# Four-layer graph network on one core: graph 0's masks on VectorE, its attention rows made by TensorE, four output tiles beside the p's

## The chip, the cores and the metric

The kernel runs on one core of one Trainium2 chip. Times are device microseconds of that core. Five engines work side by side, each through its own instructions in their order: TensorE (PE, with its weight loads PEld), VectorE (DVE), ScalarE (ACT), GpSimd (POOL) and SyncE (SP, which here only issues DMAs). They wait for each other by semaphores.

## The reference

Sixteen graphs of N = 1024 nodes with D = 256 features go through four layers; `adj` is a symmetric 0/1 matrix with ones on the diagonal.

```python
    h = jnp.maximum(_layernorm(x, axis=-1), 0.0)
    x = x + _L0_gnn_ref(h, adj, L0_gnn_W, L0_gnn_a)     # and so on for layers 1 to 3

    def _L0_gnn_ref(input, adj, W, a):
        h = jnp.matmul(input, W)
        f1 = jnp.einsum('bnf,f->bn', h, a1)
        f2 = jnp.einsum('bnf,f->bn', h, a2)
        e = jax.nn.leaky_relu(f1[:, :, None] + f2[:, None, :], negative_slope=ALPHA)
        logits = jnp.where(adj > 0, e, NEG_BIG)
        attention = jax.nn.softmax(logits, axis=1)
        return jax.nn.elu(jnp.matmul(attention, h))
```

Layer 1 is the same with the softmax along the other axis. Layer 2 averages projected neighbours; layer 3 has four attention heads of 64 features and a normalization per head. The change touches what layers 0 and 1 do for the first graph.

## The kernel before

Two programs are in the kernel: a fast one, and a general one behind a flag that these inputs don't raise. Only the fast one runs. Each graph is a Python generator, `graph(b)`: it normalizes x (`Norm`), runs `layer0` to `layer3`, and hands its end to `tail`. The generators yield planned times. A queue at the end of the program always resumes the one whose planned time is least, with 120 us between graphs, and so sets the order in which the instructions are traced. From that order a planner with its own idea of durations makes each engine's order: it may put an instruction that it takes to be ready ahead of earlier ones. `later(...)` pins an instruction behind what was traced before it on its engine. All SP loads and rows are pinned.

Every layer treats nodes in NT = 8 tiles of 128.

- **Norm** (L599 to L681): statistics on VectorE (L631, or sums from `residual` and squares on ScalarE, L640), 1/std on POOL (L592, L593), the normalized and clipped rows hn on ScalarE (L667), transposes on TensorE (L680, called flips here), copied to ht (L681).
- **Mask** (L548): the transposed adjacency comes as int32 pieces `raw` of 128x512, 256 KB each, three buffers, sixteen pieces a graph, loaded by SP (L566). ScalarE squares each into bytes and sums it (L575).
- **layer0** (L742): eight projections of 258 columns (L686), copied to hs on ScalarE (L746). The last two columns are f1 and f2 of each node. The f1's, one per partition, must become a row that stands in all 128 partitions: `column` gathers them on VectorE (L717), `spread` transposes them on TensorE (L699), takes the exps (L703) and writes them to DRAM (L705), and `everywhere` reads them back with a broadcast (L711). Layer 0 needs two such rows (scales 1 and 0.2). Then come the eight p's: two VectorE operations over 128x1024 each (L769 and L771, the second with the mask), a reciprocal, and hs scaled by it on ScalarE (L773). Output tile i needs all eight p's: eight products (L759) into one PSUM bank. EARLY = 2 tiles are multiplied beside the p's, and up to p 6 their products are pinned; the other six tiles follow. For each tile ScalarE takes exp and a copy (L791, L793) and VectorE adds to x (L736, L737).
- **layer1** (L798) is alike, with one row, one VectorE operation per p (L822), products of 257 columns (L815), and e and v in L838 and L840.
- **layer2** and **layer3**: products L877, L883 and L942; p's L929.

PSUM has four pools of two banks: tr (transposes), mm (projections, weight preparation), at (output tiles of layers 0 and 1), hd (output tiles of layers 2 and 3). The SBUF tag `e` has two buffers.

The loads that graph 0 does not need at once wait behind its p's: `behind(t)` copies one element of the p that was traced last (`gates[-1]`, L484) into the tile to be loaded. `more()` traces them in three steps: the weights of layer 1 (`weights01`, with a small preparation on TensorE, L507, and copies L511), of layer 2 with the biases (L521 scales beta on VectorE), and of layer 3 (L534 to L536). The x of graphs 1 and 2 waits in the same way.

Of the kernel before, what the change touches and what calls it, by code (L numbers as in the profile page):

```python
# [8 lines left out]
F32 = mybir.dt.float32  # L9
U8 = mybir.dt.uint8  # L10
AF = mybir.ActivationFunctionType
OP = mybir.AluOpType
AX = mybir.AxisListType

P = 128
# [406 lines left out]
def tile_simple_stack(  # L422
# [11 lines left out]
    nc = tc.nc  # L434
    B, N, D = x.shape
# [4 lines left out]
    HALF = 512  # L440
    NHALF = N // HALF
    PER = NT // NHALF
    EIGHTH = 128
    NE = N // EIGHTH
    S, S3 = 0.2, 0.01
# [3 lines left out]
    EARLY = 2  # L449

    const = ctx.enter_context(tc.tile_pool(name="const", bufs=1))
# [9 lines left out]
    ident = const.tile([P, P], F32)  # L461
    make_identity(nc, ident)
    neg_half = const.tile([P, NT * H], F32)
    nc.vector.memset(neg_half, -0.5)
    unread = const.tile([P, D], U8)

    state = ctx.enter_context(tc.tile_pool(name="state", bufs=2))
    work = ctx.enter_context(tc.tile_pool(name="work", bufs=2))
# [24 lines left out]
    wx, rows = {}, {}  # L493
# [54 lines left out]
    class Mask:  # L548
# [4 lines left out]
        def __init__(self, b):  # L553
            self.b, self.next, self.raws = b, 0, []
            self.bytes = None
            for _ in range(self.AHEAD):
                self.load()
# [11 lines left out]
        def step(self, count=1):  # L569
            if self.bytes is None:  # L570
                self.bytes = state.tile([P, NT, N], U8, tag="mask", name="mask")
            for _ in range(count):
                s, n, g, raw = self.raws.pop(0)
                k = self.b * NT * NHALF + s
                nc.scalar.activation(  # L575
                    self.bytes[:, n, g * HALF : (g + 1) * HALF], raw, AF.Square, accum_out=squares[:, k : k + 1]
                )
                self.load()

    def load_adj(b, g):  # L580
# [108 lines left out]
    def new_hs(name="hs"):  # L689
        return state.tile([P, NT, W3], F32, tag="hs", name=name, bufs=3)  # L690

    def spread(col, n, scales, name):

        k = n * NT
        ps = tr_ps.tile([P, P], F32, tag="tr", name="ps_col")
        nc.tensor.transpose(ps[:k, :], col, ident)  # L699
        all_rows = []  # L700
        for scale in scales:
            e = small.tile([H * NT, P], F32, tag="e_row", name="e_row", bufs=2)
            nc.scalar.activation(e[:k, :], ps[:k, :], AF.Exp, scale=scale)  # L703
            d = dram.tile([n, N], F32, tag=f"row_{name}", name="d_row", bufs=4)
            later(nc.sync.dma_start(d.rearrange("r (t p) -> (r t) p", p=P), e[:k, :]))  # L705
            all_rows += [d[r] for r in range(n)]
        return all_rows

    def everywhere(d, tag):
        row = work.tile([P, N], F32, tag=tag, name="row", bufs=2)  # L710
        later(nc.sync.dma_start(row, d.partition_broadcast(P)))  # L711
        return row

    def column(src, n):

        col = small.tile([P, H, NT], F32, tag="col", name="col", bufs=2)
        nc.vector.tensor_copy(col[:, :n, :], src.rearrange("p t n -> p n t"))  # L717
        return col[:, :n, :].rearrange("p n t -> p (n t)")
# [22 lines left out]

    def layer0(b, xs, m, norm, after):  # L742
        hs = new_hs()
        for n in range(NT):
            ps = project(norm, wx[0], n, D + 2)
            nc.scalar.activation(hs[:, n, : D + 2], ps[:, : D + 2], AF.Copy, scale=norm.rs[n])  # L746
            m.step()
            yield 0.98
        mask = m.bytes
        row_a, row_b = [everywhere(d, "row") for d in spread(column(hs[:, :, D : D + 1], 1), 1, (1.0, S), "l0")]  # L750
        q = small.tile([P, NT], F32, tag="q", name="q")
        nc.scalar.activation(q, hs[:, :, D + 1], AF.Exp, scale=1.0 - S)
        watch(b, 0, hs[:, :, D : D + 2])
        yield 5.42
        ps_ = []
        early = [at_ps.tile([P, HALF], F32, tag="at", name="ps_o0") for _ in range(EARLY)]

        def product(ps, i, j):
            m = nc.tensor.matmul(  # L759
                ps[:, :D], ps_[j][:, i * P : (i + 1) * P], hs[:, j, :D], start=(j == 0), stop=(j == NT - 1)  # L760
            )
            if i < EARLY and j < 7:
                later(m)

        for j in range(NT):
            if m.raws:
                m.step(2)
            p = weights("p0")
            nc.vector.scalar_tensor_tensor(p, row_a, q[:, j : j + 1], row_b, op0=OP.mult, op1=OP.max)  # L769
            z = small.tile([P, 2], F32, tag="z", name="z", bufs=8)  # L770
            nc.vector.scalar_tensor_tensor(p, p, 1.0, mask[:, j, :], op0=OP.mult, op1=OP.mult, accum_out=z[:, 0:1])  # L771
            nc.vector.reciprocal(z[:, 1:2], z[:, 0:1])
            nc.scalar.activation(hs[:, j, :D], hs[:, j, :D], AF.Copy, scale=z[:, 1:2])  # L773
            ps_.append(p)
            if b == 0:
                gates.append(p)
            for i, ps in enumerate(early):
                if j:
                    product(ps, i, j - 1)
            yield 2.7  # L780
        for i, ps in enumerate(early):
            product(ps, i, NT - 1)
        for i in range(NT):
            if i < EARLY:
                ps = early[i]
            else:
                ps = at_ps.tile([P, HALF], F32, tag="at", name="ps_o0")
                for j in range(NT):
                    product(ps, i, j)
            e = work.tile([P, D], F32, tag="e", name="e")  # L790
            nc.scalar.activation(e, ps[:, :D], AF.Exp)  # L791
            v = work.tile([P, D], F32, tag="v", name="v")
            nc.scalar.copy(v, ps[:, :D])  # L793
            residual(xs, i, v, after, e)
            yield 3.74


    def layer1(b, xs, mask, norm, after):  # L798
        hs = new_hs()
        for n in range(NT):  # L800
            ps = project(norm, wx[1], n, D + 2)
            nc.scalar.activation(hs[:, n, : D + 2], ps[:, : D + 2], AF.Copy, scale=norm.rs[n])
            yield 1.05
        (d_row,) = spread(column(hs[:, :, D + 1 : D + 2], 1), 1, (S - 1.0,), "l1")
        row = everywhere(d_row, "row")
        watch(b, 1, hs[:, :, D : D + 2])
        q = small.tile([P, NT], F32, tag="q", name="q")
        nc.scalar.activation(q, hs[:, :, D], AF.Exp, scale=1.0 - S)
        nc.scalar.activation(hs[:, :, D], hs[:, :, D], AF.Exp, scale=S)
        yield 8.0  # L810
        ps_ = []
        early = [at_ps.tile([P, HALF], F32, tag="at", name="ps_o1") for _ in range(EARLY)]

        def product(ps, i, j):
            nc.tensor.matmul(  # L815
                ps[:, : D + 1], ps_[j][:, i * P : (i + 1) * P], hs[:, j, : D + 1], start=(j == 0), stop=(j == NT - 1)
            )

        for j in range(NT):
            nc.scalar.activation(hs[:, j, :D], hs[:, j, :D], AF.Copy, scale=hs[:, j, D : D + 1])  # L820
            p = weights("p1")
            nc.vector.scalar_tensor_tensor(p, row, q[:, j : j + 1], mask[:, j, :], op0=OP.max, op1=OP.mult)  # L822
            ps_.append(p)
            for i, ps in enumerate(early):
                product(ps, i, j)
            yield 1.35
        for i in range(NT):
            if i < EARLY:
                ps = early[i]
            else:  # L830
                ps = at_ps.tile([P, HALF], F32, tag="at", name="ps_o1")
                for j in range(NT):
                    product(ps, i, j)
            k = b * NT + i
            z = shares[:, k : k + 1]
            nc.vector.reciprocal(z, ps[:, D : D + 1])
            e = work.tile([P, D], F32, tag="e", name="e")
            nc.scalar.activation(e, ps[:, :D], AF.Exp, scale=z)  # L838
            v = work.tile([P, D], F32, tag="v", name="v")
            nc.scalar.activation(v, ps[:, :D], AF.Copy, scale=z)  # L840
            residual(xs, i, v, after, e)
            yield 3.74
# [186 lines left out]
    def loads(b):  # L1029
        loaded[b] = load_x(b)  # L1030
        yield 30.0
        masks[b] = Mask(b)
        yield 0
# [3 lines left out]
    def more():  # L1037

        weights01(1, w1, w1_t, a1, (1, 0))
        yield 21.6  # L1040
        weights2()
        yield 9.2
        weights3()
        yield 0
# [2 lines left out]
    next(loads_0)  # L1047
    weights01(0, w0, w0_t, a0, (0, 1), wait=False)
    next(loads_0)
    queue = [(36, 0, more())] + [(b * APART, b, graph(b)) for b in range(B)] + [(b * APART - 60, b, loads(b)) for b in range(1, B)]  # L1050
    while queue:
        queue.sort(key=lambda g: g[:2])
        at, b, g = queue.pop(0)
# [86 lines left out]
```

## Time and profile before

| | |
|---|---|
| median of 3 runs | 2623.5 us (2618.03 to 2626.04) |
| span of the profiled execution | 2619.6 us |
| TensorE busy | 2456.4 us, 94% |
| VectorE, ScalarE busy | 1965.3 us (75%), 1439.9 us (55%) |
| TensorE busy in the first 156 us | 109.9 us |
| TensorE busy in 313 to 470 us | 152.8 us of 157 |
| mean granted TensorE clock | 0.986 |

The span runs from the first to the last instruction of one execution taken by the profiler; the page gives no other time of that execution, and its span lies inside the runs' own spread. A line of the timeline gives the start, how long the instructions took, engine, line and operation, what is written and read, and how often; in brackets the engine's idle time before it and what ended that. A busy TensorE means that instructions are in it, not that it is at its best: their ends are modelled.

### The profile page before, as it was taken

Reading aid. Unit: us, or ns where it says so; the run is one execution under the profiler, and the core shown is the slowest. Engines: PE = TensorE matmul, PEld = TensorE weight load, DVE = VectorE, ACT = ScalarE, POOL = GpSimd, SP = SyncE. Lnnn points to the kernel's source line nnn. Section 1 sums busy time; section 2 is a strip of 40 time slices with the busy share of each in tenths; the row PEclk is TensorE's granted clock in tenths of the full one; section 3 lists DMA queues with packets and bytes.
Section 4 is the critical chain, followed back from the end, with each engine's and each line's share of the span. In section 5 each row is a group of like instructions: output and inputs, shape, how many; then the busy total and the mean of one; then the engine's idle time right before and its main releaser. Section 6 shows DMA issues by size and latency. Waiting matters only on the chain.

```text
span 2619.6 us, 63024 instructions
## 1 busy us (share of the span) xinstructions
PE 2456.4 (94%) x26194; PEld 2094.9 (80%) x26194; DVE 1965.3 (75%) x3815; ACT 1439.9 (55%) x4065; POOL 449.5 (17%) x454
## 2 busy tenths in 40 slices
PE   5799999999999999999999999999999999999975
PEld 4688888888878888787888878888888888878864
DVE  4457778687687977778687787877778687787858
ACT  4564755637565473755637565473755637565350
POOL 1010211203112030211203112030211203011021
PEclk8899999999999999999999999999999999999997
DMA  4541442616225251331615225251432615224021
GB/s 144 126 85 54 107 85 62 133 59 144 53 76 126 70 133 55 108 83 62 134 58 144 57 76 122 70 133 54 124 67 64 137 59 140 66 71 101 26 65 36
DMA packets 212632, 233.76 MB, mean 89 GB/s; under 512 B 10416, under 2 KB 161072, under 8 KB 212336
## 3 DMA queue, kind: packets, MB, share of 16 engines
q1 hardware_dynamic: 74608, 145.73, 17.5%
q0 software_dynamic: 137728, 83.90, 17.5%
q8 instruction: 208, 3.41, 0.5%
q14 instruction: 88, 0.72, 0.1%
HBM read 212.35 MB, written 17.24 MB: 88 GB/s over the span
## 4 chain that ended last, share of the span: by engine, by line
PE 56%; DVE 16%; DMA 12%; ACT 11%; issue 3%; POOL 2%; SPq 0%; DVEq 0%; POOLq 0%; ACTq 0%
PE ps_o L759 15%; PE ps_proj L686 12%; PE ps_o L942 9%; DVE p L929 6%; PE ps_o L883 6%; PE ps_o L815 6%; DMA row<-d_row 5%; PE pt_h L680 5%; DMA raw<-in_adj_t 4%; DVE p L822 4%; ACT mask L575 3%; PE ps_o L877 3%; ACT hn L667 2%; DMA d_row<-e_row 2%; ACT unread L640 2%
## 5 line engine op out<-in xcount | busy, mean ns | idle before, releaser
L929 DVE SCALAR_TENSOR_TENSOR p<-row,q,mask 128x1024 f32<-128x1024 f32 x512 | 631.9, 1278 | 65.4 <-PE ps_o L942 55.7
L942 PEld LDWEIGHTS ps_o<-hb,p 128*64 128x64 f32 x16384 | 505.5, 138 | 102.0 <-DVE p L929 41.2
L942 PE MATMUL ps_o<-hb,p 128*64 128x65 f32 x16384 | 541.6, 224 | 28.9 <-DVE p L929 20.8
L759 PE MATMUL ps_o<-hs,p 128*128 128x256 f32 x2048 | 494.0, 386 | 26.4 <-ACT hs L773 26.0
L686 PE MATMUL ps_proj<-wx,ht 128*128 128x258 f32 (+2 forms) x2048 | 507.8, 388 | 4.0 <-ACT hs L746 2.3
L815 PE MATMUL ps_o<-hs,p 128*128 128x257 f32 x2048 | 494.3, 388 | 14.5 <-ACT mask L575 7.7
L759 PEld LDWEIGHTS ps_o<-hs,p 128*128 128x128 f32 x2048 | 379.7, 191 | 82.8 <-ACT hs L773 30.3
L815 PEld LDWEIGHTS ps_o<-hs,p 128*128 128x128 f32 x2048 | 373.9, 190 | 69.9 <-ACT mask L575 8.3
L686 PEld LDWEIGHTS ps_proj<-wx,ht 128*128 128x128 f32 x2048 | 365.8, 190 | 79.6 <-ACT hs L746 10.4
L592 POOL TENSOR_SCALAR rs<-mv 128x4 f32<-128x4 f32 (+1 forms) x112 | 40.6, 362 | 1555.3 <-ACT unread L640 1542.1
L593 POOL TENSOR_TENSOR rs<-rs,neg_half 128x4 f32<-128x4 f32 (+2 forms) x144 | 261.6, 1818 | 11.7
L736 DVE SCALAR_TENSOR_TENSOR xs<-e,xs 128x256 f32<-128x256 f32 x256 | 108.0, 422 | 182.2 <-ACT e L791 134.1
L667 ACT ACTIVATE hn<-xs,shift 128x256 f32<-128x256 f32 x384 | 175.3, 502 | 123.6 <-DVE shift L635 123.6
L680 PE MATMUL pt_h<-ident,hn 128*128 128x128 f32 x1024 | 180.9, 287 | 43.4 <-ACT hn L667 42.4
L575 ACT ACTIVATE mask<-raw 128x512 uint8<-128x512 int32 x256 | 160.1, 627 | 86.7 <-DMA raw<-in_adj_t 59.5
L883 PE MATMUL ps_o<-hi,adj 128*128 128x258 f32 x1024 | 202.9, 321 | 1.6
L680 PEld LDWEIGHTS pt_h<-ident,hn 128*128 128x128 f32 x1024 | 115.1, 142 | 111.1 <-ACT hn L667 95.0
L585 POOL DMA_DIRECT2D adj<-in_adj x128 | 114.6, 896 | 480.3 <-PE ps_o L883 478.6
L737 DVE SCALAR_TENSOR_TENSOR xs<-v,xs 128x256 f32<-128x256 f32 x384 | 161.0, 422 | 29.5 <-ACT v L793 16.2
L769 DVE SCALAR_TENSOR_TENSOR p<-row,q 128x1024 f32<-128x1024 f32 x128 | 161.4, 1270 | 25.1 <-DMA row<-d_row 25.1
L950 ACT ACTIVATE res<-ps_o 128x260 f32<-128x260 f32 x128 | 46.5, 375 | 228.0 <-PE ps_o L942 227.7
L822 DVE SCALAR_TENSOR_TENSOR p<-row,q,mask 128x1024 f32<-128x1024 f32 x128 | 156.9, 1279 | 10.3 <-DMA row<-d_row 10.1
(108 smaller groups left out, 3000.1 us busy)
## 6 DMA issues: line engine op xcount, KB each, us to landing
raw<-in_adj_t SPq DMA_DIRECT2D x256, 256.0 KB
adj<-in_adj POOLq DMA_DIRECT2D x128, 512.0 KB, 4.9
row<-d_row SPq DMA_DIRECT2D x112, 512.0 KB
xs<-in_x POOLq DMA_DIRECT2D x32, 512.0 KB, 7.1
out<-xs SPq DMA_DIRECT2D x32, 512.0 KB
wx<-in_w SPq DMA_DIRECT2D x3, 256.0 KB
d_row<-e_row SPq DMA_DIRECT2D x48, 4.0 KB
wts<-in_w_t SPq DMA_DIRECT2D x2, 256.0 KB
```

What stands on the lines that cost most here:

```text
L575: nc.scalar.activation(self.bytes[:, n, g * HALF : (g + 1) * HALF], raw, AF.Square, accum_out=squares[:, k : k + 1])
L593: nc.gpsimd.tensor_tensor(rs[:, :n], rs[:, :n], neg_half[:, :n], op=OP.pow)
L667: nc.scalar.activation(hn, xs[:, 2 * g + k, :], AF.Relu, scale=scale, bias=bias)
L680: nc.tensor.transpose(pt[:, c, k * P : (k + 1) * P], hn[:, c * P : (c + 1) * P], ident)
L686: nc.tensor.matmul(ps[:, :width], norm.ht[:, c, n * P : (n + 1) * P], w[:, c, :width], start=(c == 0), stop=(c == DC - 1))
L759: m = nc.tensor.matmul(ps[:, :D], ps_[j][:, i * P : (i + 1) * P], hs[:, j, :D], start=(j == 0), stop=(j == NT - 1))
L769: nc.vector.scalar_tensor_tensor(p, row_a, q[:, j : j + 1], row_b, op0=OP.mult, op1=OP.max)
L815: nc.tensor.matmul(ps[:, : D + 1], ps_[j][:, i * P : (i + 1) * P], hs[:, j, : D + 1], start=(j == 0), stop=(j == NT - 1))
L822: nc.vector.scalar_tensor_tensor(p, row, q[:, j : j + 1], mask[:, j, :], op0=OP.max, op1=OP.mult)
L883: nc.tensor.matmul(ps[:, : D + 2], adj_n[j][:, i, :], h[:, i, : D + 2], start=False, stop=(h is lo and i == NT - 1), skip_group_check=True,)
L929: nc.vector.scalar_tensor_tensor(p, row, q[:, jj, h : h + 1], mask[:, jj, :], op0=OP.max, op1=OP.mult)
L942: nc.tensor.matmul(pss[g][part, k * HW : (k + 1) * HW], ps_[t][:, i * P : (i + 1) * P][:, part], hbv[:, j + t, h, :], start=(j == 0 and t ...
```

## The change

Five edits, all for the first graph. (1) Its masks are made by VectorE, as raw times raw with the sum alongside. (2) Its rows in layers 0 and 1 are made without DRAM: for each node tile a diagonal matrix, identity times f, goes through TensorE with a matrix of ones as weights, which puts the f's into every partition in PSUM; ScalarE takes the exps out of two PSUM banks of pool hd into `row`. (3) In layers 0 and 1 two more output tiles, in the banks of hd, are multiplied beside the p's. In layer 0 the pinning covers them too. (4) A 128x128 matrix of ones is set at the start. (5) `more()` starts at 58 instead of 36 in planned time.

```diff
+    ones = const.tile([P, P], F32)
+    nc.vector.memset(ones, 1.0)
...
-                nc.scalar.activation(
-                    self.bytes[:, n, g * HALF : (g + 1) * HALF], raw, AF.Square, accum_out=squares[:, k : k + 1]
-                )
+                to, total = self.bytes[:, n, g * HALF : (g + 1) * HALF], squares[:, k : k + 1]
+                if self.b == 0:
+                    nc.vector.scalar_tensor_tensor(to, raw, 1.0, raw, op0=OP.mult, op1=OP.mult, accum_out=total)
+                else:
+                    nc.scalar.activation(to, raw, AF.Square, accum_out=total)
...
+    class Row:
+        def __init__(self):
+            self.ps = [hd_ps.tile([P, HALF], F32, tag="hd", name="ps_row") for _ in range(NHALF)]
+
+        def add(self, n, f):
+            g, k = divmod(n, PER)
+            diag = work.tile([P, D], F32, tag="e", name="diag")[:, :P]
+            nc.vector.tensor_scalar(diag, ident, f, None, op0=OP.mult)
+            nc.tensor.matmul(self.ps[g][:, k * P : (k + 1) * P], ones, diag, start=True, stop=True)
+
+        def rows(self, scales):
+            made = [work.tile([P, N], F32, tag="row", name="row", bufs=2) for _ in scales]
+            for g in range(NHALF):
+                for row, scale in zip(made, scales):
+                    nc.scalar.activation(row[:, g * HALF : (g + 1) * HALF], self.ps[g], AF.Exp, scale=scale)
+            return made
...
     def layer0(b, xs, m, norm, after):
         hs = new_hs()
+        by_pe = Row() if b == 0 else None
         for n in range(NT):
             ps = project(norm, wx[0], n, D + 2)
             nc.scalar.activation(hs[:, n, : D + 2], ps[:, : D + 2], AF.Copy, scale=norm.rs[n])
+            if by_pe:
+                by_pe.add(n, hs[:, n, D : D + 1])
             m.step()
             yield 0.98
         mask = m.bytes
-        row_a, row_b = [everywhere(d, "row") for d in spread(column(hs[:, :, D : D + 1], 1), 1, (1.0, S), "l0")]
+        if by_pe:
+            row_a, row_b = by_pe.rows((1.0, S))
+        else:
+            row_a, row_b = [everywhere(d, "row") for d in spread(column(hs[:, :, D : D + 1], 1), 1, (1.0, S), "l0")]
...
         early = [at_ps.tile([P, HALF], F32, tag="at", name="ps_o0") for _ in range(EARLY)]
+        if b == 0:
+            early += [hd_ps.tile([P, HALF], F32, tag="hd", name="ps_o0") for _ in range(NHALF)]
...
-            if i < EARLY and j < 7:
+            if i < len(early) and j < 7:
                 later(m)
...
-            if i < EARLY:
+            if i < len(early):
                 ps = early[i]
...
-    queue = [(36, 0, more())] + [(b * APART, b, graph(b)) for b in range(B)] + [(b * APART - 60, b, loads(b)) for b in range(1, B)]
+    queue = [(58, 0, more())] + [(b * APART, b, graph(b)) for b in range(B)] + [(b * APART - 60, b, loads(b)) for b in range(1, B)]
```

`layer1` is changed as `layer0` is: `by_pe.add(n, hs[:, n, D + 1 : D + 2])` in its projections, one row with the scale S - 1, the two tiles more in `early`, and `i < len(early)` in the loop over the tiles.

## The prediction

> **What bounds the kernel now.** First the windows view in steps of one graph's period, to see where TensorE is not the bound.
>
> ```profile
> span 2619.6 us, 63024 instructions
> PE 2456.4 (94%) x26194; PEld 2094.9 (80%) x26194; DVE 1965.3 (75%) x3815; ACT 1439.9 (55%) x4065; POOL 449.5 (17%) x454
> PEclk8899999999999999999999999999999999999997
> ```
>
> ```profile
> 0.00:156.00 156.00, 109.92 (x469) 86.20 (x470) 59.70 (x209) 84.57 (x229) 17.76 (x28) 0.89 0.45 113
> ...
> 470.00:627.00 157.00, 152.03 (x1637) 130.01 (x1636) 122.19 (x235) 89.74 (x257) 28.18 (x28) 1.00 0.37 92
> 627.00:784.00 157.00, 152.12 (x1637) 129.95 (x1636) 122.28 (x235) 89.73 (x255) 28.25 (x28) 1.00 0.38 92
> ...
> 2196.00:2353.00 157.00, 152.86 (x1641) 130.69 (x1641) 122.44 (x237) 90.61 (x258) 28.15 (x28) 1.00 0.36 93
> ```
>
> The columns are PE, PEld, DVE, ACT, POOL, then clock. From 156 us on every 157 us stretch holds 152 us of matmuls: TensorE is the bound and the pattern repeats. In the first 156 us it idles 46 us. All edits concern graph 0, so only those 46 us are in play. Next, who waited in the first 160 us (total, times, longest):
>
> ```profile
> PE ps_o L759 <- ACT hs L773: 14.1, 2, 13.1
> ...
> PE ps_wa L507 <- DMA avs<-in_a: 10.7, 2, 7.1
> ...
> DVE p L769 <- DMA row<-d_row: 8.0, 1, 8.0
> PE ps_o L815 <- ACT mask L575: 7.7, 1, 7.7
> ...
> DVE p L822 <- DMA row<-d_row: 6.5, 1, 6.5
> ...
> DVE row_beta L521 <- DMA row_beta<-in_beta: 3.2, 1, 3.2
> ```
>
> Then the timeline around the first gap:
>
> ```profile
> 28.83 0.68 SPq L705 DMA_DIRECT2D d_row<-e_row  x2
> ...
> 30.07 0.82 SPq L711 DMA_DIRECT2D row<-d_row  x2
> 30.93 0.42 SPq L566 DMA_DIRECT2D raw<-in_adj_t  x1
> 35.53 2.48 DVE L769 SCALAR_TENSOR_TENSOR p<-row,q 128x1024 f32<-128x1024 f32 x2 [7.96 <-DMA row<-d_row]
> 36.05 0.63 ACT L575 ACTIVATE mask<-raw 128x512 uint8<-128x512 int32 x1 [6.47 <-DMA raw<-in_adj_t]
> ```
>
> The last hs of layer 0 is done at 27.3 us; the row goes to DRAM and comes back; the first p begins at 35.5. The last adjacency piece is queued on SP behind the rows (30.93), so its mask ends only at 36.6. TensorE starts its products at 41.0. Layer 1 repeats this: hs done at 97.7, p at 104.5, products at 106.0 (the wait the profile puts on L575 is one for that p, on DVE).
>
> [...]two dependent DMAs cost 6.7 us from 28.8 to 35.5. [...]the granted clock is 0.50 in 100-110 us, after the 8 us gap, and the eight records from 40.97 take 3.78 us where later ones take 0.23 us each. [...]a matmul waiting for a DMA holds those behind it, as L507 did at 46.9-50.5 us.
>
> **The change part by part**, on the clock of the profiled execution. Its span is 2619.6, 3.9 us below the median of the runs, 2623.5; differences carry over.
>
> *Masks of graph 0 from ScalarE to VectorE.* ScalarE loses 16 x (0.63 + 0.19) = 13.1 us, all but one in 9-30 us, where it is 90% busy (9.13 and 8.90 of 10). VectorE gains 16 operations over 512 columns. This form is not in the trace; between 0.42 us at 256 columns (L737) and 1.21 us at 1024 (L771) it is 0.69, plus 0.08 for the accumulator: 0.77, in all 12.3 us. VectorE is busy 2.7 us of 10-30, so there is room. But the masks may stand between the statistics that release rs: four of them delay rs by 3.1 us, from 14.4 to 17.5. The hs copies began at 20.04, held by masks on ScalarE, so this delay fits under what was removed. Then TensorE must still do six projections (5.85 us in the trace) and most of the ones products. I leave the end of hs at 27.3; bounds 26 and 30.
>
> *Rows made by TensorE.* Removed per row: a column copy, a transpose, exps, the write, the broadcast, and SP's queue is free for the adjacency. Added per layer: eight diag operations on VectorE (0.15 us at 1 column, 0.295 at 256: 0.22 each), eight ones products, and the exps: four of 128x512 from PSUM in layer 0, two in layer 1. The nearest row for these is L681, 0.58 us. A float32 product is two records here (L759 counts 2048 for 1024 products); L680's 128 columns give 0.29 a record alone and PEld 0.19. I take 0.35 us a product (0.25 to 0.55), 2.8 us a layer, on TensorE's path. After the last hs in layer 0: diag 0.22, product 0.35, two exps 1.16 (the first half's can run earlier), handovers 0.3: row at 29.3, not 35.5. **6.2 us** less. The 3-deep raw loads land 2 to 3 us after issue and are consumed sooner now, so I expect the last near 27.
>
> *The p stage.* Eight p's need 8 x 2.5 = 20 us of VectorE (1.27 + 1.21 + 0.08 + reciprocal, overlapped starts). Before: 35.5 to 56.3, of which 0.9 was L511 waiting for L507. I allow 0.6 for a late mask: last p at 49.9, its scaled hs at 50.6, against 57.0. 6.4 us less.
>
> *Four early tiles.* TensorE's share per p grows from 0.93 to 1.86 us at full clock, below the 2.5 us of a p. After the last p: four products 1.9, then four tiles instead of six, 4 x 3.72 = 14.9. Flips of the normalized rows 2.5 and L507, moved here, 1.9 (eight records took 1.84, twice). The weights' loads now all start behind the last p: wx1, its transpose and avs ahead of wx2, biases and beta on SP, with 1 MB of x on POOL. Landings were 2.3 us light and 6 us loaded. avs can hold TensorE, beta can hold VectorE longer than its 3.2, since 0.5 MB more is ahead of it; but VectorE late by some us has two tiles of slack. I put 2.0 (0 to 6) for both; before, the beta wait cost 2.7 us idle. End: 50.6 + 1.9 + 14.9 + 2.5 + 1.9 + 2.0 = 73.8, against 88.3: **14.5 us** less. L534's 2.6 us, in that stage before, come later behind layer 1: +2.6.
>
> *Layer 1.* Ones products +2.8. From the last hs to the first product 8.3 us before; now 0.22 + 0.35 + 0.58 + 0.3, one p 1.28, 0.2: 2.9, so -5.4. [...]which saves half of 4 us: -2.0 (0 to -2). Four early tiles bring nothing here: two already fill TensorE (9.47 us busy from 105.98). Their PSUM banks are otherwise used only from layer 2 on.
>
> *Queue start 36 to 58.* It takes L507 out of the p stage, counted above; what is later is wx1, which has 20 us until layer 1.
>
> Sum at layer 2: -14.5 + 2.6 + 2.8 - 5.4 - 2.0 = **-16.5 us**. Everything afterwards is bound by TensorE and unchanged, and graph 1 is released by the last p of graph 0 and by raws that now need not wait behind layer 1's row (100.2 before). So the end moves with it: 2619.6 - 16.5 = 2603.1 in a profile, 2607.0 as a median.
>
> **Rivals.**
> (a) *Graph 1 does not follow.* Its x is gated by the last p, only 6.4 us earlier, and its raws wait on SP behind a3s, whose buffer of tag e now queues behind the diags. Then TensorE idles at the end of layer 1 and 6 of the 16 arrive: 2617.5. Against: its x landed at 65, long before use at 130. Chance 0.10.
> (b) *The row is not earlier by what it says:* masks waiting on raws sit on VectorE ahead of the diags, so TensorE waits behind a ones product. The raw waits on ScalarE after the start were 0.5, 0.4 and 6.5. If the row slips to 34, and with the other costly ends, -9: 2614.5. Chance 0.08.
> (c) *Slower: the interleaving of later graphs gets worse.* The order on each engine is planned anew, with graph 0 further ahead of graph 1, and about 14 repeats multiply any loss. At +1.2 us per period (157 to 158.2) the gain is gone; at +2 it is 28 - 16.5 = +11.5: 2635. For it: single periods differ by more than 1 us. Against: the stretches settle to 152.0-152.9 us of PE right after graph 0. Chance 0.10.
> The forecast has 0.72.
>
> **How the numbers follow.** About 0.3%, 7.9 us, is what a measurement can tell from no change. The forecast's own range is 2602 to 2618 (bounds summed: row 26 to 30, stall 0 to 6, products 0.25 to 0.55), nearly all of it faster by over 0.3%: 0.70. Adding half of (b): 0.74 faster. Rival (a), the rest of (b) and the forecast's rim: 0.16 the same. (c): 0.10 slower. The range 2599 to 2623 leaves out (c) and a gain above 24 us.
>
> **What would show it.** Right: L769 starts near 29 us, L575 is absent before 80 us, DVE shows 128x512 int32 operations of about 0.7 us; after the last p four tiles of L759 remain and layer 1's p begin near 88 us; the clock is 1.00 through layer 1; the period stays 157. The chain of waits loses two row DMAs. Wrong: a DVE wait on raw ahead of diag, TensorE waiting for avs or VectorE for beta over 6 us, or a first L883 later than 145 us (156.4 before); or, with all these right, a longer period.

## The result and the profile after

The changed kernel takes **2610.6 us** (median of 4 runs, 2609.6 to 2613.0) against 2624.3 before in the same comparison: a ratio of **0.9949** (95% interval 0.9936 to 0.9962), 13.7 us less. The forecast was 2607.0, 16.5 less, with a range of 2599 to 2623.

The page of the changed kernel, beginning:

```profile
span 2611.1 us, 63088 instructions
PE 2462.2 (94%) x26224; PEld 2102.5 (81%) x26224; DVE 1978.2 (76%) x3862; ACT 1431.3 (55%) x4036; POOL 449.9 (17%) x454
PEclk8999999999999999999999999999999999999987
```

Its windows view, the same stretches as before (PE, PEld, DVE, ACT, POOL, clock, DMA):

```profile
0.00:156.00 156.00, 126.07 (x577) 102.13 (x578) 81.01 (x272) 83.71 (x218) 20.21 (x30) 0.92 0.48 118
...
470.00:627.00 157.00, 151.58 (x1635) 129.63 (x1633) 120.06 (x231) 88.53 (x252) 26.91 (x27) 1.00 0.35 89
627.00:784.00 157.00, 151.94 (x1635) 129.87 (x1635) 123.11 (x238) 90.23 (x256) 29.00 (x30) 1.00 0.35 91
...
2196.00:2353.00 157.00, 151.14 (x1621) 129.04 (x1620) 120.57 (x234) 88.62 (x252) 26.34 (x27) 0.99 0.36 89
```

The first 156 us hold 126 us of matmuls instead of 110: work that stood behind them has moved in. The repeating stretches hold 151 to 152 us, 0.2 to 1.7 less than the same stretches before. The first product of layer 2 stood at 156.4 us (L883, the first line) and now stands at 143.0 (L922, the second):

```profile
156.41 0.47 PE L883 MATMUL ps_o<-hi,adj 128*128 128x258 f32 x1
...
143.05 0.47 PE L922 MATMUL ps_o<-hi,adj 128*128 128x258 f32 x1
```

That is 13.4 us earlier, and the median moved by 13.7. The two figures do not come from the same executions, though. In the two profiled ones the lead over before shrinks from 13.4 us at graph 0's layer 2 to 9.8 at graph 4's, and 8.5 are left at the end. The profiled execution of before was a good one: its span, 2619.6, lay near the low end of its own runs, and it was granted a mean clock of 0.986, which only 2 of 61 later runs of before reached (median 0.983); the runs of the changed kernel had 0.986 to 0.987. How much of the 13.7 us is the earlier start and how much is a fuller clock, the record does not split. Below, medians are used for times, and traces for places.

What of the waits is left in the first 110 us of the changed kernel:

```profile
PE ps_wa L509 <- DMA avs<-in_a: 11.0, 2, 7.4
...
DVE row_beta L523 <- DMA row_beta<-in_beta: 3.9, 1, 3.9
...
DVE mask L579 <- DMA raw<-in_adj_t: 2.0, 3, 0.9
```

Both waits for a row from DRAM are gone. The first of the two avs waits is the program's start; the second, 3.65 us, now lies in layer 0's output stage. The last line is new: masks waiting on VectorE. Where they stand shows in the timeline:

```profile
11.61 0.66 DVE L579 SCALAR_TENSOR_TENSOR mask<-raw 128x512 uint8<-128x512 int32 x1
12.19 0.08 DVE L579 DVE_READ_ACCUMULATOR mask<-raw 128x1 f32 x1
...
16.58 0.69 DVE L579 SCALAR_TENSOR_TENSOR mask<-raw 128x512 uint8<-128x512 int32 x1 [0.74 <-DMA raw<-in_adj_t]
17.19 0.08 DVE L579 DVE_READ_ACCUMULATOR mask<-raw 128x1 f32 x1
17.19 0.75 DVE L635 BATCH_NORM_STATS2 st<-xs 128x6 f32<-128x256 f32 x2
...
19.66 2.08 POOL L597 TENSOR_TENSOR rs<-rs,neg_half 128x8 f32<-128x8 f32 x1
...
33.74 2.48 DVE L800 SCALAR_TENSOR_TENSOR p<-row,q 128x1024 f32<-128x1024 f32 x2 [1.62 <-ACT row L734]
```

The last packet of x ended at 10.3 us, yet the statistics of its second half (L635) run at 17.2, behind seven masks of which three waited for a raw piece. 1/std (rs) is done at 21.7 us, where it was done at 14.4 before.

### The profile page after: what moved, and what is told of

It is laid out like the page before. It is cut to its first block, busy times and chain, and to the rows that moved or that the text cites. A ratio compares the mean times of both kernels' runs of the same rounds, so it can differ in the third digit from the quotient of the medians.

```text
span 2611.1 us, 63088 instructions
## 1 busy us (share of the span) xinstructions
PE 2462.2 (94%) x26224; PEld 2102.5 (81%) x26224; DVE 1978.2 (76%) x3862; ACT 1431.3 (55%) x4036; POOL 449.9 (17%) x454
## 3 DMA queue, kind: packets, MB, share of 16 engines
q0 software_dynamic: 137728, 83.90, 17.2%
q8 instruction: 208, 3.41, 0.5%
## 4 chain that ended last, share of the span: by engine, by line
PE 57%; DVE 17%; DMA 11%; ACT 10%; issue 3%; POOL 2%; SPq 0%; DVEq 0%; POOLq 0%; ACTq 0%
PE ps_o L790 16%; PE ps_proj L690 12%; PE ps_o L981 10%; DVE p L968 6%; PE ps_o L922 6%; PE ps_o L854 5%; DMA row<-d_row 5%; PE pt_h L684 5%; DVE p L861 4%; DMA raw<-in_adj_t 4%; PE ps_o L916 3%; ACT mask L581 2%; DMA d_row<-e_row 2%; ACT hn L671 2%; ACT unread L644 2%
## 5 line engine op out<-in xcount | busy, mean ns | idle before, releaser
L968 DVE SCALAR_TENSOR_TENSOR p<-row,q,mask 128x1024 f32<-128x1024 f32 x512 | 632.3, 1280 | 66.9 <-PE ps_o L981 55.7
L790 PEld LDWEIGHTS ps_o<-hs,p 128*128 128x128 f32 x2048 | 379.5, 191 | 75.0 <-ACT hs L804 23.2
L854 PEld LDWEIGHTS ps_o<-hs,p 128*128 128x128 f32 x2048 | 375.3, 191 | 62.9 <-DVE p L861 10.3
L922 PE MATMUL ps_o<-hi,adj 128*128 128x258 f32 x1024 | 203.2, 321 | 1.6
L581 ACT ACTIVATE mask<-raw 128x512 uint8<-128x512 int32 x240 | 150.1, 626 | 69.7 <-DMA raw<-in_adj_t 42.8
L760 DVE SCALAR_TENSOR_TENSOR xs<-v,xs 128x256 f32<-128x256 f32 x384 | 161.4, 423 | 29.4 <-ACT v L824 16.5
L922 PEld LDWEIGHTS ps_o<-hi,adj 128*128 128x128 f32 x1024 | 152.5, 190 | 14.2 <-ACT hi L908 4.8
```

What stands on the lines that cost most here:

```text
L581: nc.scalar.activation(to, raw, AF.Square, accum_out=total)
L760: nc.vector.scalar_tensor_tensor(x, v, 0.0, x, op0=OP.max, op1=OP.add, accum_out=after.sums[:, i % 2 : i % 2 + 1])
L790: m = nc.tensor.matmul(ps[:, :D], ps_[j][:, i * P : (i + 1) * P], hs[:, j, :D], start=(j == 0), stop=(j == NT - 1))
L854: nc.tensor.matmul(ps[:, : D + 1], ps_[j][:, i * P : (i + 1) * P], hs[:, j, : D + 1], start=(j == 0), stop=(j == NT - 1))
L922: nc.tensor.matmul(ps[:, : D + 2], adj_n[j][:, i, :], h[:, i, : D + 2], start=False, stop=(h is lo and i == NT - 1), skip_group_check=True,)
L968: nc.vector.scalar_tensor_tensor(p, row, q[:, jj, h : h + 1], mask[:, jj, :], op0=OP.max, op1=OP.mult)
```

## The experiments

Every kernel below is the changed kernel with one edit or several, timed against the kernel before. By their intervals, two ratios that differ by less than some 0.002 (5 us) cannot be told apart. "Layer 2" is the start of its first product in graph 0, in one profiled execution each; the loads at the start alone shift such a place by some 1.5 us (rs was done at 21.7 to 23.2 us in kernels that do not differ up to there).

| kernel | ratio to before, 95% | layer 2, us |
|---|---|---|
| before | 1 | 156.4 |
| changed | 0.9949 (0.9936 to 0.9962) | 143.0 |
| masks on ScalarE | 0.9947 (0.9931 to 0.9964) | 141.3 |
| rows through DRAM | 0.9997 (0.9987 to 1.0006) | 159.7 |
| two early tiles in both layers | 0.9985 (0.9977 to 0.9994) | 152.4 |
| four in layer 0 only | 0.9948 (0.9932 to 0.9964) | 146.4 |
| four in layer 1 only | 0.9963 (0.9950 to 0.9975) | 151.4 |
| weights' queue start 36 | 0.9964 (0.9951 to 0.9976) | 149.4 |
| statistics first | 0.9927 (0.9912 to 0.9942) | 137.0 |
| loads at 36, preparation at 58 | 0.9931 (0.9915 to 0.9948) | 137.7 |
| both repairs | **0.9908** (0.9893 to 0.9924) | 137.7 |
| both, beta later | 0.9913 (0.9899 to 0.9927) | 138.9 |
| both, layer 3's weights later | 0.9913 (0.9898 to 0.9928) | 135.1 |
| rows through DRAM, layer 3's weights later | 0.9952 (0.9938 to 0.9966) | 146.9 |

The two last columns go together: the ratio times 2624.3 us, less the place of layer 2, lies between 2462 and 2469 us in all fourteen rows. In single executions the time from layer 2 to the end varies more, from 2459 to 2475 us. The last two rows flatter the place by some 2.5 us: there twelve records of projections, which the other kernels have ahead of layer 2's first product, come behind it.

**Masks back on ScalarE.**

```diff
-                if self.b == 0:
+                if self.b < 0:
```

> The changed kernel with graph 0's masks back on ScalarE, all else kept. Theory: on VectorE the masks stand between the statistics of the first and second half of x and wait there for raw pieces, so that 1/std came at 21.7 us instead of 14.4 and the row at 33.7. With the masks on ScalarE 1/std is back at 14.4, the row comes at about 30.5 and the end is 3 us earlier than in the changed kernel (ratio to before about 0.9937). Rival: ScalarE, 90 percent busy with the masks in 10 to 30 us, is what holds the hs copies, and the ones products hold TensorE; then the row comes at 34 to 36 and the end is 0 to 3 us later (0.995 to 0.996).

Measured: rs at 14.9 us, first p at 30.8 instead of 33.7, layer 2 at 141.3, and a ratio that cannot be told from the changed kernel's. The place is what the theory said, 2.9 us at the row; the 3 us in time that it expected are less than these times can show. The move of the masks to VectorE, in the order that it got, brought nothing that shows.

**Statistics first.** The same masks on VectorE, traced behind the statistics:

```diff
             norm.pair(xs, g)
-            m.step()
+            if b:
+                m.step()
             yield 2.55
+        if b == 0:
+            m.step(NT // 2)
...
+                    made = nc.vector.scalar_tensor_tensor(to, raw, 1.0, raw, op0=OP.mult, op1=OP.mult, accum_out=total)
+                    if s < self.AHEAD:
+                        later(made)
```

> The changed kernel with graph 0's first masks traced behind the statistics of all of x and the first three pinned there, still on VectorE. Theory: what took 4 us of the row's gain is only the order on VectorE (statistics behind masks that wait for raw). 1/std then comes at 14.5 to 15.5 us as before instead of 21.7, the row at 29 to 30 instead of 33.7, and the end is 3 to 5 us earlier than in the changed kernel (ratio to before 0.993 to 0.994). Rival: the raws, consumed from 12.4 us on, now hold the diags, so the row comes at 32 to 34 and the time is the same as in the changed kernel (0.995).

From the timeline of this kernel:

```profile
12.10 0.24 DVE L638 BATCH_NORM_AGGREGATE mv<-st 128x2 f32<-128x6 f32 x2
...
12.45 0.68 DVE L579 SCALAR_TENSOR_TENSOR mask<-raw 128x512 uint8<-128x512 int32 x1
...
13.28 2.00 POOL L599 TENSOR_TENSOR rs<-rs,neg_half 128x8 f32<-128x8 f32 x1
...
27.42 1.29 DVE L802 SCALAR_TENSOR_TENSOR p<-row,q 128x1024 f32<-128x1024 f32 x1
```

The statistics end at 12.3, rs at 15.3, the first p is at 27.4: earlier than in the changed kernel by 6.3 us, in layer 2 by 6.0, in time by some 5.8 (0.9927 against 0.9949, at the limit of what can be told). The theory holds for the row: the order on VectorE cost it 6.3 us. Not all of that went straight through: four of the masks now stand between the first p's, so that the last hs is 3.9 us earlier; the rest came in the output stage, 2.2 us shorter in this execution, with 3.4 us of half clock instead of 6.8. Against the masks on ScalarE the first p is 3.4 us earlier and layer 2 4.3; so masks on VectorE are worth having once the order is mended, as far as the traces go.

**Rows through DRAM again.**

```diff
-        by_pe = Row() if b == 0 else None
+        by_pe = None
```

> The changed kernel with the rows of graph 0 through DRAM again in layers 0 and 1. Theory: this part is worth the two round trips less the ones products. Layer 0: the row at 37 to 38 instead of 33.7, layer 1: first p 4 us later relative to its last hs and the clock halved again (2 us). First product of layer 2 at 151 instead of 143.0, end 8 us later than in the changed kernel (ratio to before 0.998). Rival: the round trips are hidden or repaid by the ones products' time on TensorE, at most 3 us later (0.996).

Measured: first p of layer 0 at 39.1 (expected 37 to 38), and in layer 1 6.5 us from the last hs to the first p instead of 1.8 (expected 4 us more). But layer 2 starts at 159.7 and the whole gain is gone: 12.6 us by the ratios, where the theory had 8. From layer 1's first p, at 99.8, to layer 2 it took some 60 us, in the changed kernel 50.9. TensorE's timeline there:

```profile
101.28 2.05 PE L854 MATMUL ps_o<-hs,p 128*128 128x257 f32 x4 [7.30 <-DVE p L861]
103.26 1.02 PE L536 MATMUL ps_wa<-a3s,w3ts 64*128 64x10 f32 x4
104.22 1.23 PE L854 MATMUL ps_o<-hs,p 128*128 128x257 f32 x2
105.37 1.03 PE L536 MATMUL ps_wa<-a3s,w3ts 64*128 64x10 f32 x4
```

and its windows view:

```profile
100.00:120.00 20.00, 18.72 (x47) 13.05 (x48) 11.28 (x24) 8.36 (x24) 0.00 (x0) 0.51 0.68 200
```

TensorE is busy 18.7 of 20 us, at a granted clock of 0.51: 47 matmul records instead of the usual 80 or more. L536, the preparation of layer 3's weights, which queue start 58 has put between layer 1's products, lies among them until 114.9. It is not one execution's chance: the mean granted clock was 0.981 to 0.983 in all 14 runs of this kernel, and 0.986 to 0.987 in those of the changed one. This calls for an experiment of its own.

**Rows through DRAM, and layer 3's weights later**, so that L536 comes behind layer 1's p stage:

```diff
         weights2()
-        yield 9.2
+        yield 45.0
```

> The changed kernel with rows through DRAM, as before in the run that undid that part, and in addition the weights of layer 3 traced at 125 instead of 89, so that their small products (64 rows, 10 columns) no longer lie between those of layer 1's p stage. In that run TensorE was at half clock for 23.9 us there, though busy for 18.4 of them, and the clock came back 5 us after the last small product. Theory: [...]Without them the half clock ends within 7 us of layer 1's first product and the end is 4 to 7 us earlier than in that run (ratio to before 0.9975). Rival: the long half clock came from the gap or from chance; then it stays over 10 us and the ratio 0.999 to 1.000.

Its TensorE timeline and the same window:

```profile
99.34 19.82 PE L854 MATMUL ps_o<-hs,p 128*128 128x257 f32 x80 [7.31 <-DVE p L861]
...
122.62 0.61 PE L536 MATMUL ps_wa<-a3s,w3ts 64*128 64x10 f32 x4
```

```profile
100.00:120.00 20.00, 19.92 (x85) 16.51 (x84) 12.77 (x37) 7.52 (x23) 0.00 (x0) 0.91 0.20 54
```

The gap ahead is as long (7.31 us), and half clock lasts to 103.7, some 4.4 us from the first product. Layer 2 starts at 146.9, 12.8 us earlier (some 2.5 of it by the order of the projections), and the ratio is 0.9952 instead of 0.9997; the five runs had a mean clock of 0.984 to 0.986. Moving layer 3's weights took away both the long half clock and the loss. The edit moves more than the eight small products: the loads and copies of these weights go with them, and five of graph 1's adjacency pieces are issued by 100 us instead of fifteen by 117, so that the DMA share in the window falls from 0.68 to 0.20. That the transfers held the clock down is a rival, and the changed kernel's trace speaks against it:

```profile
91.08:94.49 3.41, 1.75 (x12) 1.22 (x10) 2.37 (x6) 3.40 (x9) 0.00 (x0) 1.00 0.69 225
94.49:97.90 3.41, 3.41 (x10) 2.36 (x10) 1.83 (x6) 2.22 (x7) 0.00 (x0) 0.50 0.39 109
97.90:107.90 10.00, 10.00 (x49) 8.61 (x49) 6.87 (x13) 5.36 (x15) 0.00 (x0) 1.00 0.61 201
```

Ten microseconds at 201 GB/s went by at full clock. What the length goes with is worked out in the last section.

Against the changed kernel (0.9949), the rows through DRAM now cost nothing that the times can tell. So the rows made by TensorE are worth much less by themselves than undoing them alone suggests. That their second use is to keep the gap ahead of the small products short is my reading of these runs; no kernel varied the gap alone.

**Two early tiles again, in both layers, then in one at a time.**

```diff
-        if b == 0:
+        if b < 0:
             early += [hd_ps.tile([P, HALF], F32, tag="hd", name="ps_o0") for _ in range(NHALF)]
```

(and the same for `ps_o1`).

> The changed kernel with two early tiles in graph 0 again, the banks of hd unused there. Theory: two tiles of 3.7 us more after the last p in layer 0, of which the wait for avs (3.65 us, in which TensorE has nothing else to do in its order) is not filled: 6 to 7.5 us later than in the changed kernel, nothing from layer 1 (ratio to before 0.9975). Rival: VectorE's wait for beta is the bound of that stage whatever TensorE does, then 0 to 3 us later (0.995 to 0.996).

> The changed kernel with four early tiles in layer 0 and two in layer 1. With two in both layers the end was 11.6 us later than in the changed kernel; layer 0 gave 4 us of that, and from layer 1's first p to the first product of layer 2 it took 56 us instead of 51, with TensorE at half clock for 10 us from 98 us on though always busy. Theory: two tiles in layer 1 leave TensorE so thin beside the p's that the clock stays halved; so about 5 us later than in the changed kernel (0.997) and half clock for 10 us or more in layer 1. Rival: the long half clock was chance of that execution or came from the later start; then the same as the changed kernel (0.995) and half clock for 3.4 us in layer 1.

> The changed kernel with two early tiles in layer 0 and four in layer 1. Theory as for the one with four in layer 0 alone: the rest of the 11.6 us is here, 4 to 7 us later than in the changed kernel (0.997), and the half clock in layer 1 lasts 3.4 us. Rival (the whole loss belongs to layer 0 and its later start): 10 to 12 us later (0.9985) with the long half clock again.

Measured: 0.9985 with two in both, some 9.5 us above the changed kernel, where 6 to 7.5 were expected. Four in layer 0 alone give the changed kernel's time (0.9948); four in layer 1 alone give 0.9963, 3.7 us more, which is within the noise. So the four extra tiles together are worth some 9.5 us (give or take 4 by the intervals), and the times do not say how these divide. The traces say something on layer 1. From its first product to layer 2, with two tiles there (first line) and with four (the changed kernel, second line):

```profile
91.60:146.35 54.75, 51.05 (x225) 41.03 (x225) 23.61 (x90) 39.24 (x107) 4.21 (x6) 0.91 0.21 65
...
93.46:143.02 49.56, 48.08 (x224) 38.44 (x225) 22.81 (x90) 38.88 (x107) 4.25 (x6) 0.97 0.23 72
```

TensorE idles 3.7 us with two tiles and 1.5 with four; both kernels with two tiles there have 3.7, and all seven with four tiles, rows by TensorE and the small products among them have 1.5. The rest of the difference is half clock (10.2 us against 3.4). My guess that two tiles in layer 1 keep the clock halved fell with the third kernel: it has four there and half clock for 13.7 us, busy for 13.6 of them. The changed kernel, with the same layer 1, has 3.4 us. With the small products between, the length of the half clock differs that much between traces, and so they cannot split the 9.5 us further.

**Queue start 36 again.**

```diff
-    queue = [(58, 0, more())] + ...
+    queue = [(36, 0, more())] + ...
```

> The changed kernel with the weight loads' queue start at 36 again. Theory: the wait for avs moves from the output stage, where TensorE is the bound (3.65 us, then half clock for 3.4 us or more), into the p stage between p 3 and p 4, where TensorE has about 1 us of slack per pair of p's: 2 to 4 us earlier than in the changed kernel (0.9937). Rival: the pinned products behind it are delayed by the whole wait and VectorE waits for its copies, so that it is 2 us later than in the changed kernel (0.9957).

Measured: 0.9964, 3.9 us above the changed kernel, which is within the noise; but the gain that the theory forecast is excluded (0.9937 lies outside the interval). The rival fits in size but not in mechanism. The wait for avs in the p stage was only 1.9 us, and the last hs was ready 55.8 - 35.2 = 20.6 us after the first p, as in the changed kernel (20.2). What came instead is in the waits of that kernel:

```profile
PE pt_h L684 <- ACT hn L671: 12.4, 4, 5.5
...
DVE row_beta L523 <- DMA row_beta<-in_beta: 6.3, 1, 6.3
```

VectorE waits 6.3 us for beta in the output stage, the normalized rows come late, and TensorE stands for 5.5 us at a flip; L536 is also back in that stage. It ends 32.3 us after the last hs, in the changed kernel 26.4. That beta is the cause was not tried in this kernel.

**Loads at 36, preparation at 58**: the weights of layer 1 are fetched behind p 3, and their products come behind the pinned ones.

```diff
         later(nc.sync.dma_start(avs, a.rearrange("(c p) k -> p c k", p=P)))
+        yield
         for fc in range(DC):
...
-        weights01(1, w1, w1_t, a1, (1, 0))
+        first = weights01(1, w1, w1_t, a1, (1, 0))
+        next(first)
+        yield 22.0
+        list(first)
...
-    weights01(0, w0, w0_t, a0, (0, 1), wait=False)
+    list(weights01(0, w0, w0_t, a0, (0, 1), wait=False))
...
-    queue = [(58, 0, more())] + ...
+    queue = [(36, 0, more())] + ...
```

> The changed kernel with layer 1's weights loaded at queue time 36 (behind p 3) and their TensorE preparation traced at 58. Theory: TensorE's wait for avs behind the last p (3.65 us) and the half clock after it (6.8 us, some 3 us lost) go, nothing takes their place because TensorE still has tiles to multiply: 5 to 7 us earlier than in the changed kernel (0.9925). Rival: VectorE's wait for beta, 3.9 us, is the one that sets the end of the stage and comes last with or without avs: at most 2 us earlier (0.994).

Measured: 0.9931, 4.7 us less than the changed kernel (just within the noise), and layer 2 at 137.7, 5.3 us earlier. The avs wait behind the last p is gone, the half clock at 60 us too, and the output stage takes 19.8 us instead of 26.4. VectorE's wait for beta grew to 5.5 us and did not take over: TensorE waits 0.5 us at a flip.

**Both repairs**, alone, with beta's scaling later, and with layer 3's weights later:

> Both repairs together: statistics ahead of the masks, and layer 1's weights loaded behind p 3 but prepared at 58. Theory: each takes away its own wait on graph 0's path, so the gains add: first product of layer 2 at about 132 us (137.0 and 137.7 with one of them, 143.0 with neither), ratio to before 0.991. Rival: VectorE's wait for beta (3.9 us in the changed kernel, 5.0 and 5.5 with one repair), which lands no earlier, becomes the bound of layer 0's output stage; then layer 2 starts at 135 to 137 and the ratio stays at 0.9925.

> The two repairs, and the scaling of beta on VectorE traced 40 us of planned time later and pinned there. Theory (beta's wait hides behind the tiles that TensorE still has): the same as without it within 1 us of the first product of layer 2. Rival (beta's wait is the bound): 3 us earlier than the kernel with the two repairs alone, 0.1 percent of the time.

```diff
-        nc.vector.tensor_scalar(rows["beta3"], rows["beta3"], -2.0, None, op0=OP.add)
...
         weights3()
+        yield 40.0
+        later(nc.vector.tensor_scalar(rows["beta3"], rows["beta3"], -2.0, None, op0=OP.add))
```

> The two repairs, and the weights of layer 3 traced at 125 instead of 89. Theory: with the row made by TensorE the gap ahead of layer 1's first product is 3 us and the half clock there only 3.4 us, so that little is to be had: 0 to 2 us earlier than the two repairs alone, the small products being done at full clock among others. Rival: moving them behind the raws of graph 1 on SP delays graph 1 or layer 3: 2 us later or more.

In time the two repairs give 0.9908, or 2603.6 us, and 10.8 us (by the ratios) below the changed kernel. That is the sum of the two gains; but the intervals leave open how much the second adds to the first. The trace does not show the sum: layer 2 at 137.7, as with one repair. In that execution the first p was late (30.4 instead of 27.4), half clock in layer 1 lasted 6.8 us, and TensorE waited 1.6 us at flips in the stage where VectorE waited for beta. That wait of 5.8 us

```profile
DVE row_beta L524 <- DMA row_beta<-in_beta: 5.8, 1, 5.8
```

costs nothing that shows in time: without it the ratio is 0.9913. In the traces it costs some 2 us: from the last hs to the projections of layer 1 it took 20.7 us with it and 18.7 without, and the waits at flips fell from 1.6 us to 0.3, which is nearer to the rival than to the theory. Layer 2 did not start earlier for that (138.9), because half clock in layer 1 lasted 13.7 us in this execution, which was the slowest of its five runs (2615.6 us against 2601.1 to 2607.1). Moving layer 3's weights on top gives 0.9913, no difference either way.

## Why the prediction was right, step by step

Its main argument holds: TensorE bounds everything after graph 0's start, and a head start at the first product of layer 2 arrives at the end, by the medians of all fourteen kernels to within some 4 us either way. Rival (c), a worse interleaving of later graphs, did not come; rival (a) neither: graph 1's first product of layer 2 is at 297.5 instead of 310.0, and raws of graph 1 were issued at 90.7 instead of 100.2. The forecast was close as a sum, and less so in its terms:

| change of the moment | predicted | measured |
|---|---|---|
| first p of layer 0 | -6.2 | 35.5 to 33.7: -1.8 |
| last scaled hs | -6.4 | 57.0 to 53.9: -3.1 |
| end of layer 0's products | -14.5 | 88.6 (read as 88.3) to 80.3: -8.3 |
| first product of layer 1 | -17.1 (-14.5 + 2.8 - 5.4) | 106.0 to 93.5: -12.5 |
| first product of layer 2 | -16.5 | 156.4 to 143.0: -13.4 |

- **The row of layer 0** is the step that failed most. The masks' price was right (0.66 to 0.69 and 0.08 us, predicted 0.69 and 0.08). "Four of them delay rs by 3.1 us" was not: seven stand in front of the last statistics, and three of these wait for their raw, together 2.0 us; rs slipped by 7.3. I had counted the busy time of four masks, and neither the other three nor their waits, though the planner, as said above, goes by its own idea of what is ready. Rival (b) had the wait and the row's time (34), but put it at the diags.
- **The p stage** took 20.2 us from first p to last scaled hs, predicted 21.3.
- **The output stage** took 26.4 us, predicted 23.2. The term that was too small is the stall, 2.0: TensorE waited 3.65 us for avs and then ran 6.2 us at half clock, some 3 us lost. The halved clock after a wait was in the part on layer 1 and missing here. The beta wait was rightly given slack: 5.0, 5.5 and 5.8 us of it went with 0, 0.5 and 1.6 us of TensorE's waiting at flips; with 6.3 us it was 5.5.
- **Layer 1**: from the last hs (90.4) to the first product (93.5) 3.1 us, predicted 2.9. The ones products lengthened the projections by 1.0 us (from the end of layer 0's products to the last hs 10.1 us, before 9.1), predicted 2.8.
- **From there to layer 2** the prediction had +0.6 (L534 moved here 2.6, full clock -2.0) and -0.9 was measured. Full clock did not come: half clock took 3.4 us of busy time (before 4.0), which saves 0.3. That "four early tiles bring nothing here" was wrong too: TensorE idled 1.5 us instead of 4.2. L536 came back as foreseen, but the longer half clock that went with it (18.4 us busy against 4.4 in the two kernels with rows through DRAM) was not.

So two terms that gave more than it had (the ones products by 1.8 us, the tiles of layer 1 by some 2) made up for part of what the row, the stall and the clock lost. That the sum came within 3.1 us at layer 2 is to that extent luck. Of its signs of being right, the 0.7 us operations on VectorE, the four tiles left after the last p, the two row DMAs gone and the period (156.5 us in the mean, 156.2 before) came; the first p near 29 us, layer 1's near 88 and a clock of 1.00 through layer 1 did not.

That full clock would last through layer 1, behind a gap of 2.9 us, was the author's assumption. It did not hold: in the changed kernel the clock fell at 94.5 us, with no gap over 0.94 us in the ten before, and TensorE busy for 1.75 of the last 3.41 us. In the four traces where large products stand alone at the start of layer 1, full clock was back after 3.4 to 4.4 us of work; with the small ones between them it took from 3.4 to 18.4.

## What to carry to other kernels

Where one engine is the bound in a repeating part, time is to be found in the fill, and the start of the first full stage shows there what a part is worth, with two cautions: single executions differ by microseconds, and a changed order can move work behind that start. When work moves to an idle engine, look at what it is queued in front of and which transfer it waits for: here the order alone decided whether the move brought nothing or some 6 us at the row. Issue a load long before its consumer, and place the consumer apart from it; moving both together only moves the wait (for avs 3.65 us in the output stage with queue start 58, 1.9 us in the p stage with 36, and none in either with the loads at 36 and the products at 58).

## What was not expected of the hardware

TensorE stayed at half clock while it was busy. Ten traces have layer 3's eight small products (64 rows, 10 columns) between layer 1's first ones. In these, the half clock there lasted 3.4 us (four traces), 6.8, 10.2 (two), 13.7 (two) and 23.9 us, nearly all of it busy (18.4 us in the last). In the four traces that have no small products there (before, queue start 36, and the two with layer 3's weights later) TensorE was busy for 3.4 to 4.4 us of it. One pair of kernels differs in when layer 3's weights come, with 18.4 and 4.4 us.

The traces show what the length goes with. In those of before and of the changed kernel all changes of the clock lie on one grid of 3.41 us. Count for each step of this grid the columns that matmul records stream (the second number of what they read: 257 for a record of layer 1's products, 10 for a small one; a record across an edge is shared out by time). In these two traces, from the first record of the clock (17.8 and 16.0 us) to layer 2, half clock followed each of the 17 steps with at most 1116 columns, and full clock each of the 62 steps with at least 1566; no step lay between. In the changed kernel the step before the fall has 655, and the next one, itself at half clock, 1566; then the clock is full. With rows through DRAM, the steps from 95.8 us on have 0, 657, 951, 1249, 1385, 1278 and 2061 columns, and then the clock is full; with layer 3's weights moved, 0, 412 and 2068. So a step can be busy from end to end and still be followed by half clock, as those with 1249, 1385 and 1278 columns were: the small products fill its time and stream few columns. What makes 3.4 or 13.7 us of it in kernels that are alike was not shown. The count was made after the runs, and no kernel was made to test it; it tells only of the float32 products of this stretch.
